# A two-layer block: where the zeros of the expert slots are written, when the 4-bit weights are loaded, and in which order the first sequence goes

## The chip, the core and the metric

The kernel runs on one core of a Trainium2 chip. A core has five engines that run their own instruction streams in order: PE (matrix multiplication), DVE (vector), ACT (activation functions and copies), POOL (general), and SP, which here only issues transfers. Transfers between the chip's main memory and the on-chip memory are carried by 16 DMA engines. An instruction waits where it depends on another engine's or a transfer's result, and everything behind it on its engine waits with it.

The metric is the device time of one execution, in microseconds (us), lower is better.

## The reference

Four sequences of 256 tokens with 256 features go through two layers. Cut to what matters:

```python
# layer 0
x = x + attn0(layernorm(x))      # 16 heads of 16, window of 128, RMS-normalised q and k, rope
x = x + ffn0(layernorm(x))       # weights (1024 x 256 and 256 x 1024) from 4 bits:
                                 #   (q - 7.5) * scale per block of 64, plus a rank-16 product (LoRA)
# layer 1
x = x + scan(layernorm(x))       # selective state space: h_t = exp(dt*A) h_(t-1) + dt*B*x, 16 states
x = x + moe_block(layernorm(x))  # attention with 32 query heads of 128 and 4 key/value heads,
                                 #   then 32 experts, 8 for each token, and a shared expert
```

All arithmetic is float32, apart from some small bf16 operands that hold a value in parts. A sequence's steps depend on each other in that order; the sequences depend on each other only in the expert stage, where tokens are ordered by expert.

## The kernel before

**Streams.** Each piece of the work is a Python generator that yields after a small step: `l0_attention(b)` (24 steps: 4 of projection, 8 that find each row's lowest score, 10 of softmax and values, and the close), `dequantise` (8 pieces that build the feed-forward's float32 weights), `feed_forward(b)` followed by `scan(b)` (together 25 steps for a sequence, `after[b]`), `lower()` (layer 1's attention over all sequences, 16 pairs of heads each, 64 steps) and `zeros()` (35 steps). `timed(stream, start, span, steps)` gives each stream a due time and a pace, and `play` always takes the step that is due first. Times in `timed` are plain numbers that only order the steps; they are not microseconds.

**Planner.** The order in which `play` writes the instructions is a priority. The framework's planner then goes through them with its own model of durations and puts on each engine, at each moment, the instruction of the highest priority that is ready by that model. So an instruction that waits for nothing can be placed far ahead of its place in the program. Buffers come from pools: a tile with `bufs=n` has n buffers in turn, and the next user waits until the last reader is done. Waits are put in by the framework.

**Stages.** First `play`: layer 0's attention of sequence 0 (`first`) and `dequantise` must end, and sequence 1's attention (`second`, `heads[1]`) may advance beside them. Its pool `deq` holds sequence 0's attention buffers and the LoRA factors; when it closes, its memory goes to the pools of layer 1's attention (`l1`) and of the scan (`ssm`), so their first users wait for it. Then the constants of the second layer are loaded (lines 957 to 974). The second `play` (line 1057) holds all else up to the experts: `after[b]`, the attention of sequences 1 to 3 in layer 0 (`heads[1]`, `following(2)`, `following(3)`), `lower()` and `zeros()`. `lower()` runs `after[0]` to its end before its first step, and `after[b + 1]` before it opens the next sequence. Its steps load query weights (`wq`, three buffers) and output weights (`wo`, four).

**Zeros.** The experts work on slots in main memory: 32 x 1024 rows of 289 floats, where each token's row is scattered, and three arrays of sums. All must hold zero before. `zeros()` writes one expert's slots, 1,156 KB, per step, from a tile of 128 x 289 zeros whose rows are repeated by the access pattern. The tile has one buffer, and each step asks for it anew and clears it on POOL (line 706), so each clearing waits until the transfer before it has read the tile. POOL also masks layer 0's probabilities (`l_pr`, lines 362 and 366), adds the rotated parts of queries and keys (302, 567), and scales part of layer 1's probabilities (652).

**Dequantisation.** For each of four pieces of the up weights and four of the down weights, the integers and the scales (broadcast over 64 rows, two transfers) are loaded into two of the eight buffers `g2`, which all of the layer 0 code shares; DVE combines them (lines 219 and 232), PE forms the low-rank product, and DVE adds it.

**Experts.** After the last attention result (line 715 of sequence 3), rows are scattered, a plan is made, and 76 tiles go through a fixed software pipeline (`experts`); then the sums are added. The change doesn't touch this.

Of the kernel before, what the change touches and what calls it, by code (L numbers as in the profile page):

```python
# [8 lines left out]
F32 = mybir.dt.float32  # L9
I32 = mybir.dt.int32  # L10
# [6 lines left out]
P = 128  # L17
# [20 lines left out]
NE = 32  # L38
# [5 lines left out]
ROW = D + NE + 1  # L44
SUMS = 3
PAIRS = NH // 2
# [5 lines left out]
def block_kernel(ctx: ExitStack, tc, out, a):  # L52
    nc = tc.nc
    V, A, G, T = nc.vector, nc.scalar, nc.gpsimd, nc.tensor
# [5 lines left out]
    l1w = ctx.enter_context(tc.tile_pool(name="l1w", bufs=1, side="left"))  # L60
# [8 lines left out]
    def g2(name, dtype=F32):  # L69

        return gen.tile([P, 512], dtype, tag="g2", name=name)

    def halves(t):
        return t.rearrange("p (t d) -> p t d", t=2)
# [31 lines left out]
    for c in (1, 3):  # L106
        G.affine_select(
            out=masks[:, c * P : (c + 1) * P], in_=masks[:, c * P : (c + 1) * P],
# [93 lines left out]
    def dequantise(deq):  # L202
        up_a = load(deq, a["upaT"], [16, D], "up_a")
        up_b = load(deq, a["upb"], [16, FF], "up_b")
        dn_a = load(deq, a["dnaT"], [16, FF], "dn_a")
        dn_b = load(deq, a["dnb"], [16, D], "dn_b")
        dnq = a["dnq"].rearrange("(c p) d -> p c d", p=P)
        dns = a["dns"].rearrange("(c j) d -> j c d", j=2)
        for c in range(2):
            for h in range(2):  # L210
                cols = slice(h * 512, (h + 1) * 512)
                q, s = g2(f"upq{c}_{h}", I32), g2(f"ups{c}_{h}")
                nc.sync.dma_start(out=q, in_=a["upq"][c * P : (c + 1) * P, cols])
                for j in range(2):
                    nc.sync.dma_start(
                        out=s[j * 64 : (j + 1) * 64, :],
                        in_=a["ups"][2 * c + j, cols].partition_broadcast(64),
                    )
                V.scalar_tensor_tensor(s, q, -7.5, s, ALU.add, ALU.mult)
                pl = ps(f"lora_up{c}_{h}")  # L220
                T.matmul(pl, up_a[:, c * P : (c + 1) * P], up_b[:, cols], start=True, stop=True)
                V.tensor_tensor(w_up[:, c, cols], s, pl, ALU.add)
                yield
        for k in range(4):
            q, s = halves(g2(f"dnq{k}", I32)), halves(g2(f"dns{k}"))
            nc.sync.dma_start(out=q, in_=dnq[:, 2 * k : 2 * k + 2, :])
            for j in range(2):
                nc.sync.dma_start(
                    out=s[j * 64 : (j + 1) * 64, :, :],
                    in_=dns[j][2 * k : 2 * k + 2, :].partition_broadcast(64),  # L230
                )
            V.scalar_tensor_tensor(s, q, -7.5, s, ALU.add, ALU.mult)
            pl = halves(ps(f"lora_dn{k}"))
            for i in range(2):
                r = 2 * k + i
                T.matmul(pl[:, i, :], dn_a[:, r * P : (r + 1) * P], dn_b, start=True, stop=True)
            V.tensor_tensor(w_dn[:, 2 * k : 2 * k + 2, :], s, pl, ALU.add)
            yield
# [450 lines left out]
    def project1(h0, po, oT, wo):  # L689
        for i in range(2):  # L690
            for t in range(2):
# [4 lines left out]
                    skip_group_check=True,  # L696
                )

    def zeros():

        fills = [slots[e * CAP : (e + 1) * CAP, :] for e in range(NE)]
        fills += [t[:, :] for t in sums]
        for i, dst in enumerate(fills):
            n = dst.shape[0] // P
            z = l1w.tile([P, ROW], F32, tag="zero", name=f"zero{i}")
            G.memset(z, 0.0)  # L706
            nc.sync.dma_start(
                out=dst.rearrange("(p k) d -> p k d", k=n),
                in_=z[:, 0 : dst.shape[1]].unsqueeze(1).to_broadcast([P, n, dst.shape[1]]),
            )  # L710
            yield

# [193 lines left out]
    def timed(stream, start, span, steps):  # L906

        return [stream, start, span / steps]
# [36 lines left out]
    with tc.tile_pool(name="deq", bufs=1, side="left") as deq:  # L945
        l0_set(deq)
        l0_set(l0)
        first = l0_attention(0)
        ready = dequantise(deq)
        second = l0_attention(1)  # L950
        play(
            [timed(first, 0, 24, 24), timed(ready, 1, 24, 9)],
            [timed(second, 14, 24, 24)],
        )

    wx_dram = a["wxT"].rearrange("(c p) n -> p c n", p=P)
# [56 lines left out]
    def following(b):  # L1013

        for i in range(1, b):
            drained(heads[i])
        yield from heads[b]

    def lower():
        pairs = attention()  # L1020
        drained(after[0])
        for b in range(B):
            for i in range(PAIRS):
                if i == OPEN_AT // 2 and b + 1 < B:
                    drained(after[b + 1])
                if b == B - 1 and i == 0:
                    early.close()
                    scans.close()
                    wres = ctx.enter_context(tc.tile_pool(name="wres", bufs=1, side="right"))
                    end.append(ctx.enter_context(tc.tile_pool(name="end", bufs=1, side="right")))  # L1030
                    wgu.append(wres.tile([P, 2, NE, 2 * P], F32, tag="wgu", name="wgu"))
                if b == B - 1:
                    for c in range(2):
                        for k, w in ((0, "Wg"), (1, "Wu")):
                            nc.sync.dma_start(
                                out=wgu[0][:, c, 2 * i : 2 * i + 2, k * P : (k + 1) * P],
                                in_=a[w][i][:, :, c, :],
                            )
                    if i == PAIRS // 2:
                        sw2 = g2("shared_gu").rearrange("p (k c n) -> p k c n", k=2, c=2)  # L1040
                        for k, w in ((0, "Wsg"), (1, "Wsu")):
                            nc.sync.dma_start(
                                out=sw2[:, k], in_=a[w].rearrange("(c p) i -> p c i", p=P)
                            )
                        sdw = g2("shared_d")[:, 0:D]
                        nc.sync.dma_start(out=sdw, in_=a["Wsd"])
                        shared_w.extend((sw2[:, 0], sw2[:, 1], sdw))
                next(pairs)
                yield
        drained(pairs)  # L1050
# [5 lines left out]
    after = {b: sequence(b) for b in range(B)}  # L1056
    play(
        [
            timed(after[0], 24, 52, 25),
            timed(heads[1], 24, 30, 14),  # L1060
            timed(after[1], 76, 60, 25),
            timed(following(2), 54, 66, 24),
            timed(after[2], 150, 110, 25),
            timed(following(3), 120, 110, 24),
            timed(after[3], 270, 140, 25),
            timed(lower(), 76, 4 * 130, 4 * PAIRS),
            timed(zeros(), 26, 120, NE + SUMS),
        ]
    )

# [156 lines left out]
    for t in range(0, NT, 2):  # L1227
        two = slice(t, t + 2)
        parts = moe.tile([P, SUMS, 2, D], F32, tag="parts", name=f"parts{t}", bufs=2)
        for j in range(SUMS):  # L1230
            nc.sync.dma_start(  # L1231
                out=parts[:, j],
# [113 lines left out]
```

## Time and profile before

| | us |
|---|---|
| median of three runs (1225.37 to 1229.05) | 1225.68 |
| the profiled execution | 1224.67 |
| its span, first to last instruction | 1223.0 |
| PE busy (84% of the span) | 1030.4 |
| DVE busy (63%) | 773.1 |
| ACT busy (37%) | 448.8 |
| POOL busy (37%) | 446.6 |

The transfers move 132.9 MB, a mean of 109 GB/s. In the profile's rows `L706` is a line of the kernel, `out<-in` are names of tiles with numbers left out (`l_pr` is `l0_pr`), `x35` counts instructions, and a bracket at the end of a row gives the idle time of the engine before it and what ended it. PEclk or the last decimal columns give the granted clock of PE as a share of full speed. A wait that is put down to one releaser is the one that came last. `SPq` rows are transfers as SP issues them; where several are joined, the second number runs from the first issue to the last.

Two hand-overs in the trace help to place what follows. The 35 clearings run from 12.0 to 312.0 us, and the transfers out of the cleared tile are issued from 43.6 to 312.3. Layer 1's first query matmul runs at 287.0, its last attention result is added at 1006.1. By sequence, the additions to `x` end at 124.4, 221.7, 385.2 and 586.8 (layer 0 attention), 155.0, 312.0, 485.0 and 676.8 (feed-forward), 268.6, 422.0, 626.0 and 816.7 (scan), and 599.0, 771.5, 904.2 and 1006.1 (layer 1 attention).

### The profile page before, as it was taken

The page shows a single profiled execution, that of the slowest core. Times are in us where ns is not written, and L with a number is a line of the kernel's source. Part 1 is how long each engine was busy: PE and PEld are TensorE (multiplying, and loading weights), DVE is VectorE, ACT ScalarE, POOL GpSimd, SP SyncE. Part 2 cuts the span into 40 slices and gives each one's busy share as a digit, 9 for nine tenths or more (in the row PEclk, how much of TensorE's full clock was granted, in tenths as well). Part 3 has the DMA queues.
Part 4 walks back from the last instruction along what each step waited for, and adds up shares of the span by engine and source line. Part 5 has one row for each costly group of instructions (what it writes and reads, how often), then busy time and mean ns, then how long its engine had stood idle before and what let it go on. Part 6 is the DMA issues. An engine that isn't in the chain of part 4 may idle for free. (4 is left out here: it accounts for less than half of the span.)

```text
span 1223.0 us, 16090 instructions
## 1 busy us (share of the span) xinstructions
PE 1030.4 (84%) x4739; PEld 731.4 (60%) x4739; DVE 773.1 (63%) x2368; ACT 448.8 (37%) x1374; POOL 446.6 (37%) x509
## 2 busy tenths in 40 slices
PE   4887867788899899799999979989999995799880
PEld 2545633336555576566677757667877773677660
DVE  4634236772688873569984588886677643466662
ACT  1030133311454343364444454535454541333320
POOL 4021021011232231242244442346435635388882
PEclk8575866858889899899999989999999997799995
DMA  4667755656201010111122672123333315589876
GB/s 127 191 151 185 193 162 152 161 154 167 95 18 35 27 44 30 31 35 35 52 63 73 197 203 61 53 71 100 98 90 99 100 36 217 120 153 149 146 106 165
DMA packets 130323, 132.93 MB, mean 109 GB/s; under 512 B 10608, under 2 KB 124048, under 8 KB 130224
## 3 DMA queue, kind: packets, MB, share of 16 engines
q1 hardware_dynamic: 116208, 112.34, 32.9%
q0 software_dynamic: 14016, 19.44, 9.1%
q8 instruction: 42, 0.69, 0.2%
q14 instruction: 57, 0.47, 0.1%
HBM read 69.84 MB, written 61.90 MB: 108 GB/s over the span
## 5 line engine op out<-in xcount | busy, mean ns | idle before, releaser
L567 POOL TENSOR_TENSOR at_q_rot<-at_q_t,at_q_t 128x512 f32<-128x512 f32 x64 | 82.1, 1282 | 203.1 <-DVE at_q_t L563 138.8
L642 ACT ACTIVATE at_pr<-at_pr,at_low 128x128 f32<-128x128 f32 (+1 forms) x256 | 113.6, 445 | 70.5 <-DVE at_low L638 69.5
L1189 POOL DMA_INDIRECT sum<-mx_o,at x76 | 118.5, 1559 | 45.5 <-DVE mx_wj L1154 23.1
L693 PE MATMUL at_po<-at_wo,at_oT 128*128 128x256 f32 x512 | 130.4, 381 | 2.5 <-ACT at_oT L686 2.5
L611 PE MATMUL at_pq<-at_hT,at_wq 128*128 128x256 f32 x512 | 126.0, 386 | 1.2 <-ACT at_oT L686 0.9
L652 POOL TENSOR_SCALAR at_pr<-at_pr,at_rden 128x128 f32<-128x128 f32 x128 | 86.5, 685 | 89.6 <-DVE at_rden L647 71.0
L540 PE MATMUL sm_y<-sm_hc,ident 128*128 128x512 f32 x128 | 80.7, 733 | 35.8 <-DVE sm_hc L539 35.3
L611 PEld LDWEIGHTS at_pq<-at_hT,at_wq 128*128 128x128 f32 x512 | 96.8, 193 | 17.9 <-issue 2.8
L693 PEld LDWEIGHTS at_po<-at_wo,at_oT 128*128 128x128 f32 x512 | 93.2, 190 | 15.2 <-ACT at_oT L686 3.2
L563 DVE TENSOR_TENSOR at_q_t<-at_pq,rope 64x512 f32<-64x512 f32 x128 | 88.1, 688 | 8.6 <-POOL at_k_rot L567 6.2
L1140 PE MATMUL mx_pgu<-wgu,mx_xT 128*128 x304 | 82.1, 393 | 6.8 <-DVE mx_act L1165 2.9
L561 DVE TENSOR_TENSOR at_q_t<-at_pq,rope 128x512 f32<-128x512 f32 x64 | 44.0, 687 | 65.4 <-PE at_pq L611 64.3
L638 DVE CUSTOM_DVE_ANT_0 at_pr<-at_sc,masks 128x128 f32<-128x128 f32 (+1 forms) x256 | 77.4, 353 | 9.6 <-PE at_sc L634 7.8
L528 ACT ACTIVATE decay<-sm_dt,na 128x255 f32<-128x255 f32 x128 | 57.3, 499 | 64.2 <-DVE sm_h L534 59.5
L706 POOL MEMSET zero<- 128x289 f32 x35 | 12.0, 344 | 186.8 <-DMA slots<-zero 175.9
L676 ACT COPY at_pT<-at_pb 128x256 f32<-128x256 f32 x64 | 23.5, 367 | 154.1 <-PE at_pb L672 153.9
L853 POOL DMA_INDIRECT slots<-mo_row,mo_at x64 | 64.7, 1011 | 40.4 <-DVE plan_ti L748 20.9
L534 DVE TENSOR_TENSOR_SCAN sm_h<-decay,sm_w 128x512 f32<-128x512 f32 x64 | 78.0, 1236 | 0.7 <-ACT decay L528 0.3
L683 PE MATMUL at_pav<-at_pT,at_v 128*128 128x512 f32 x128 | 70.1, 630 | 8.9 <-DVE at_q_t L563 6.0
L634 PE MATMUL at_sc<-at_k_rot,at_q_rot 128*128 128x256 f32 x256 | 76.5, 380 | 0.0
L336 DVE CUSTOM_DVE_ANT_0 l_junk<-l_sc,masks 128x128 f32<-128x128 f32 (+1 forms) x128 | 40.8, 353 | 36.3 <-PE l_sc L329 33.3
L1188 DVE COPY mx_o<-mx_po 128x256 f32<-128x256 f32 x76 | 32.2, 424 | 48.4 <-DMA sum<-mx_o,at 32.3
(314 smaller groups left out, 2144.6 us busy)
## 6 DMA issues: line engine op xcount, KB each, us to landing
slots<-zero SPq DMA_DIRECT2D x32, 1156.0 KB
at_wq<-in_Wq_dram SPq DMA_DIRECT2D x64, 256.0 KB
at_wo<-in_Wo_dram SPq DMA_DIRECT2D x64, 256.0 KB
xg<-slots SPq DMA_DIRECT2D x76, 144.5 KB
wgu<-in_Wg_dram SPq DMA_DIRECT2D x32, 128.0 KB
wgu<-in_Wu_dram SPq DMA_DIRECT2D x32, 128.0 KB
wd<-in_Wd_dram SPq DMA_DIRECT2D x8, 512.0 KB
sum<-zero SPq DMA_DIRECT2D x3, 1152.0 KB
```

The costliest lines, as they stand in the source:

```text
L534: V.tensor_tensor_scan(hs.rearrange("p c l -> p (c l)"), da.rearrange("p c l -> p (c l)"), w.rearrange("p c l -> p (c l)"), 0.0, ALU.mult, ...
L540: T.matmul(y, ident, hc.rearrange("p c l -> p (c l)"), start=n == 0, stop=n == NS - 1)
L563: V.tensor_tensor(t2[lo : lo + 64], src[hi : hi + 64], sin[hi : hi + 64].unsqueeze(1).to_broadcast([64, n, S]), ALU.mult,)
L567: G.tensor_tensor(dst, t1, t2, ALU.add)
L611: T.matmul(pq[:, i, :], wq[:, c, i * HD : (i + 1) * HD], hT[:, c, :], start=c == 0, stop=c == 1,)
L634: T.matmul(sc[:, P : 3 * P], qT[:, i, P:S], kT[:, 0, :], start=True, stop=True)
L638: V.tensor_tensor_reduce(pr[:, cols], sc[:, cols], mask, 1.0, 3.0e38, ALU.add, ALU.min, low[:, k : k + 1],)
L642: A.activation(pr[:, cols], pr[:, cols], AF.Exp, scale=-1.0, bias=low[:, k : k + 1], accum_out=den[:, k : k + 1],)
L652: scaled.append(G.tensor_scalar(prs[i][:, cols], prs[i][:, cols], rden[:, k : k + 1], None, ALU.mult).ins)
L693: T.matmul(po[:, t, :], oT[:, i, t * P : (t + 1) * P], wo[:, i, :], start=h0 + i == 0 and t == 0, stop=h0 + i == NH - 1 and t == 1, skip_g ...
L1140: T.matmul(pgu, xT[:, c, :], wgu[0][:, c, :, :].rearrange("p e n -> p (e n)")[:, bass.ds(weights[i], 2 * P)], start=c == 0, stop=c == 1,)
L1189: G.indirect_dma_start(out=sums[i % SUMS], out_offset=bass.IndirectOffsetOnAxis(ap=at, axis=0), in_=o, in_offset=None, compute_op=ALU.add,)
```

## The change

Three things. The zero tile is made and cleared once, ahead of `zeros()`, and all 35 transfers read it; the stream comes due at 46 and no longer at 26. `dequantise` issues all 24 of its loads in its first step, into 16 tiles of its own in `deq`, and yields before it uses them; it now has 10 steps, due over 20. The due times change: `second` may begin at 12 and not 14, `after[0]` is due over 20 and not 52, `heads[1]` over 20, `lower()` from 45 and not 76, and the streams of the later sequences around that. The number and kind of all other instructions stay.

```diff
 def dequantise(deq):
...
+        parts = []
         for c in range(2):
             for h in range(2):
                 cols = slice(h * 512, (h + 1) * 512)
-                q, s = g2(f"upq{c}_{h}", I32), g2(f"ups{c}_{h}")
+                q = deq.tile([P, 512], I32, tag=f"upq{c}_{h}", name=f"upq{c}_{h}")
+                s = deq.tile([P, 512], F32, tag=f"ups{c}_{h}", name=f"ups{c}_{h}")
                 nc.sync.dma_start(out=q, in_=a["upq"][c * P : (c + 1) * P, cols])
...
+                parts.append((q, s))
+        for k in range(4):
+            q = halves(deq.tile([P, 512], I32, tag=f"dnq{k}", name=f"dnq{k}"))
+            s = halves(deq.tile([P, 512], F32, tag=f"dns{k}", name=f"dns{k}"))
+            nc.sync.dma_start(out=q, in_=dnq[:, 2 * k : 2 * k + 2, :])
+            for j in range(2):
+                nc.sync.dma_start(
+                    out=s[j * 64 : (j + 1) * 64, :, :],
+                    in_=dns[j][2 * k : 2 * k + 2, :].partition_broadcast(64),
+                )
+            parts.append((q, s))
+        yield
+        for c in range(2):
+            for h in range(2):
+                cols = slice(h * 512, (h + 1) * 512)
+                q, s = parts[2 * c + h]
                 V.scalar_tensor_tensor(s, q, -7.5, s, ALU.add, ALU.mult)
...
         for k in range(4):
-            q, s = halves(g2(f"dnq{k}", I32)), halves(g2(f"dns{k}"))
-            nc.sync.dma_start(out=q, in_=dnq[:, 2 * k : 2 * k + 2, :])
-            for j in range(2):
-                nc.sync.dma_start(
-                    out=s[j * 64 : (j + 1) * 64, :, :],
-                    in_=dns[j][2 * k : 2 * k + 2, :].partition_broadcast(64),
-                )
+            q, s = parts[4 + k]
             V.scalar_tensor_tensor(s, q, -7.5, s, ALU.add, ALU.mult)
...
+    zero = l1w.tile([P, ROW], F32, tag="zero", name="zero")
+    G.memset(zero, 0.0)
+
     def zeros():
...
-        for i, dst in enumerate(fills):
+        for dst in fills:
             n = dst.shape[0] // P
-            z = l1w.tile([P, ROW], F32, tag="zero", name=f"zero{i}")
-            G.memset(z, 0.0)
             nc.sync.dma_start(
                 out=dst.rearrange("(p k) d -> p k d", k=n),
-                in_=z[:, 0 : dst.shape[1]].unsqueeze(1).to_broadcast([P, n, dst.shape[1]]),
+                in_=zero[:, 0 : dst.shape[1]].unsqueeze(1).to_broadcast([P, n, dst.shape[1]]),
             )
             yield
...
-            [timed(first, 0, 24, 24), timed(ready, 1, 24, 9)],
-            [timed(second, 14, 24, 24)],
+            [timed(first, 0, 24, 24), timed(ready, 1, 20, 10)],
+            [timed(second, 12, 24, 24)],
...
-            timed(after[0], 24, 52, 25),
-            timed(heads[1], 24, 30, 14),
-            timed(after[1], 76, 60, 25),
-            timed(following(2), 54, 66, 24),
-            timed(after[2], 150, 110, 25),
-            timed(following(3), 120, 110, 24),
-            timed(after[3], 270, 140, 25),
-            timed(lower(), 76, 4 * 130, 4 * PAIRS),
-            timed(zeros(), 26, 120, NE + SUMS),
+            timed(after[0], 24, 20, 25),
+            timed(heads[1], 24, 20, 12),
+            timed(lower(), 45, 4 * 130, 4 * PAIRS),
+            timed(following(2), 50, 60, 24),
+            timed(after[1], 60, 64, 25),
+            timed(following(3), 120, 100, 24),
+            timed(after[2], 150, 100, 25),
+            timed(after[3], 270, 110, 25),
+            timed(zeros(), 46, 120, NE + SUMS),
```

## The prediction, made before the result was known

> **What bounds the kernel now.** I read the page's slices first, then the busy times of five stretches, then the waits, then the timeline of POOL, PE and SP inside the first 300 us. The slices (one digit for 30.6 us):
>
> ```profile
> PE   4887867788899899799999979989999995799880
> POOL 4021021011232231242244442346435635388882
> PEclk8575866858889899899999989999999997799995
> DMA  4667755656201010111122672123333315589876
> ```
>
> From slice 11 to 33 PE is full at full clock. In the first ten it has gaps, half its time at half clock, while DMA is at 0.5 to 0.7. The stretches are cut at the first query matmul of layer 1 (287.0), the opening of sequence 3's attention (842) and the last attention result (1006). Columns: length, then busy us of PE, its weight loads, DVE, ACT, POOL, then granted clock, DMA share, GB/s.
>
> ```profile
> 0.00:287.00 287.00, 209.87 (x788) 121.55 (x789) 147.65 (x415) 62.29 (x167) 51.72 (x116) 0.68 0.62 162
> 287.00:320.00 33.00, 29.22 (x143) 21.45 (x142) 15.89 (x64) 8.83 (x26) 6.68 (x11) 0.94 0.65 190
> 320.00:842.00 522.00, 476.46 (x2265) 340.39 (x2264) 391.07 (x1019) 241.47 (x742) 176.83 (x199) 0.96 0.22 65
> 842.00:1006.00 164.00, 161.80 (x807) 130.41 (x805) 100.36 (x331) 82.14 (x277) 77.53 (x92) 1.00 0.28 84
> 1006.00:1223.00 217.00, 153.02 (x741) 117.65 (x740) 118.16 (x539) 54.09 (x163) 133.90 (x92) 0.85 0.74 149
> ```
>
> Busy time by clock gives work in full-clock us: 209.9 x 0.68 = 142.7 by 287, then 27.5 + 457.4 + 161.8. So PE loses 144 us of the first 287 and only 72 of the next 719. After 287 PE bounds; before it, something else. The expert stage after 1006 is untouched by the change. What holds the front is in the waits and in the timeline:
>
> ```profile
> POOL zero L706 <- DMA slots<-zero: 175.9, 29, 15.5
> POOL l_pr L362 <- ACT l_pr L357: 61.1, 25, 8.9
> ```
>
> ```profile
> 156.32 0.34 POOL L706 MEMSET zero<- 128x289 f32 x1 [7.38 <-DMA slots<-zero]
> ...
> 163.86 0.34 POOL L706 MEMSET zero<- 128x289 f32 x1 [6.25 <-DMA slots<-zero]
> 164.15 0.63 POOL L362 TENSOR_SCALAR_AFFINE_SELECT l_pr<-l_pr 128x512 f32<-128x512 f32 x1
> ...
> 165.20 1.49 PE L378 MATMUL l_av<-l_pr,l_v 128*32 128x256 f32 x8 [6.69 <-POOL l_pr L366]
> ...
> 166.62 1.12 PE L189 MATMUL sm_pT<-ident,sm_xn 128*128 128x128 f32 x4
> ```
>
> POOL stands at a clearing of the one zero tile until the DMA before it has landed; behind it waits the mask of layer 0's softmax, behind that PE's `l_av`, and behind that, in PE's order, sequence 0's `sm_pT`, whose input was ready at 159.4. On SP (issue times):
>
> ```profile
> 43.55 11.15 SPq L707 DMA_DIRECT2D slots<-zero  x2
> ...
> 65.64 0.62 SPq L226 DMA_DIRECT2D dnq<-in_dnq_dram  x1
> ...
> 133.55 159.59 SPq L707 DMA_DIRECT2D slots<-zero  x22
> 293.24 0.62 SPq L607 DMA_DIRECT2D at_wq<-in_Wq_dram  x1
> ```
>
> The down weights queue behind zeros (the last at 93, used at 101), and the fourth query weight behind 22 of them. Sequence 0's milestones, from the rows of its residual adds: layer 0 attention 124.4, feed-forward 155.0, scan 268.6, first layer 1 query 287.0.
>
> **The change, part by part.**
>
> *Zero tile cleared once.* 34 of 35 clearings go: 34 x 0.34 = 11.6 us of POOL work and its 186.8 us of waiting (175.9 + 10.9 for the sums). POOL isn't the bound; what counts is what stood behind. I take the visible pieces: 6.7 us at `sm_pT` above; about 4 at the last softmax pair of sequence 0 (exponential done at 102.8, mask at 108.4 after a 5.64 us wait; PE filled most of it with other work, so 2 to 6).
>
> *Where the zeros go.* Their due time moves from 26 to 46, but nothing holds a zero DMA any longer, and the order here is made by readiness: the first clearing ran at 12.05 although its place is behind layer 0's first attention, and the first three query weights were issued at 111 to 118 for use at 287. So I expect all 35 on SP in one run behind the constant loads, from about 31 us (SP's 18 early loads end at 12.4; 24 + 17 issues at 0.45 are 18.5 more), not beside the attention. Each takes 0.53 on SP. Once the loads before them have drained (8.9 MB by the sizes of the issues, 33 us at the rate found next), at about 37, one zero of 1,184 kB occupied the DMA engines from 202.8 to 207.2, 4.4 us of a 7.3 us cycle: 269 GB/s. 35 x 4.4 = 154, end near 191. Query weights stand behind: by the Trainium skill, "DMA: Bandwidth & Descriptors", Queues, rings and completion order, each engine consumes descriptors in ring order, which speaks against this change. By the engines' row the first query weight lands at about 193, under the chain below and free. If zeros keep their present pace (312.3 - 43.6 over 34, 7.9 us; 7.5 away from the loads between), it lands at 37 + 35 x 7.5 = 300 and attention waits. I take 4.4, because the gap in each cycle is the very wait that goes; the other end is a rival. If SP meets a query weight among the zeros, it stands at it until `deq` is free, some 119, with the zeros behind it: half of them, 17 x 4.4 = 75, would end at 194, still free.
>
> *Quantised loads in front.* 24 DMAs, 4.2 MB, 15.6 us of engine time, are issued together; 11 of the 17 constant loads that they pass were issued from 14 to 19 and now come at about 24 to 28, the other six near 31 instead of 40 to 43. First uses are at 168 (`wx`) and 280 (`wv`): nothing, covered by 130 us. Without that cover it would be 15.6. What they give: DVE waited 1.5 us at 93 and 2.9 at 101 for down scales, with sequence 0's rotation and values behind it: about 4. Eight general buffers are no longer shared with these tiles; the 32 KB a partition that they take in `deq` are overlaid by tiles first needed after layer 0's first attention: nothing.
>
> *Chain of sequence 0 first.* Two more steps of sequence 1's attention go before sequence 0's end (12 left, not 14): two score steps at half clock, about 2 us each, +4. So layer 0 attention: 124.4 - 4 - 4 + 4, rounded down for the freed buffers, 119. Feed-forward: 30.6 us, of which PE gave about 7 to sequence 1's scores; I take 26: 145. Scan preparation, 155.0 to 193.3, is 38; less the 6.7, and half of the 6.2 in which DVE stood at sequence 1's reciprocal (wait 2.82, run 3.36): 28: 173. The 16 scan steps took 75.3, 4.7 each, with sequence 2's projection and scores among them. Undisturbed, the two steps from 198 ran at 2.3 by DVE, and at half clock PE needs 2.5: floor 40. Sequence 2 now comes due at 50, behind the chain, but sequence 1's softmax still shares PE: between 40 and 75 I take 53: 226. Opening 18.4, taken 17: attention at 243, 44 us earlier.
>
> *What comes back.* Sequence 2's work of 222 to 287 (scores 9.9, query-key 5.6, turns 3.9, values 2.1, transposes 0.6: 22.1 busy at 0.63 = 13.9) goes into the PE-bound stage. Some still fills gaps; I charge 9, at the 0.90 useful share that PE has after 287: 10. Against it, at 312 to 324 PE now loses some 6 us, with POOL at its last clearing and query weights between zeros: that goes.
>
> *The clock.* The Trainium skill, "TensorE: Matmul & The Clock Gate", Part 1, says that sustained busy time of some 3.4 us releases the half clock. Two rows from the front:
>
> ```profile
> 44.00:48.00 4.00, 4.00 (x17) 2.79 (x16) 4.00 (x20) 0.00 (x0) 0.00 (x0) 0.50 0.97 304
> 136.00:140.00 4.00, 4.00 (x17) 3.03 (x18) 1.29 (x8) 0.00 (x1) 0.00 (x0) 1.00 0.79 180
> ```
>
> By the rule the stretch from 36 to 72 would halve once its gaps close, 18 us more gain. By the row, PE was full there and still at 0.50, in matmuls of 16 rows; at 136 with 128-row ones it was at 1.00. I follow the row: no gain of clock in layer 0.
>
> *Sum.* 1223.0 - 44 + 10 - 6 = 1183.0. The profiled execution took 1224.67, 1.7 around its span; the median of the three runs, 1225.68, is 1.0 above that. So 1183.0 + 1.7 + 1.0 = **1186 us**.
>
> **Rivals.**
>
> *The wall of zeros (slower).* The planner thinks the query weights early, puts layer 1's matmuls ahead of other work in PE's order, and they stand until the zeros are through. At 7.5 us a zero that is 300 against 243: 1186 + 57 = 1243. It decides against the change once the weight lands after 243 + 40 = 283, at more than 7.0 us a zero (168 GB/s). For it: stretches with zeros moved only 149 to 190 GB/s. Against: in them the engines stood still 40% of the time. Chance 0.19.
>
> *Only the order moves.* PE bounds from 287 on, so all that is pushed out returns, and the planner already fills by readiness, so due times do little. Only the pieces of waiting are left: 4 + 4 + 6.7 + 6 = 20.7, less the 4 of the two extra steps: 1209, and up to 1222 as more of it returns. For it: PE was over 80% busy from 36 to 124. Chance 0.15, a quarter of it within 0.3%.
>
> *The front warms up.* Without gaps, and with layer 1's 128-row matmuls among layer 0's, the clock holds; attention starts near 215 with most work done: about 1150. Chance 0.12.
>
> **How the numbers follow.** The likeliest, chance 0.54, is 1186, own range 1163 to 1207 (scan 40 to 75, return 0 to 14). 0.3%, 3.7 us, is about what a measurement of this kernel can tell from no change. Faster: 0.54 + 0.12 + 0.11 = 0.77; same 0.04; slower 0.19. The range goes from beyond the warm case, 1142, to where half of the wall case is left out, 1240.
>
> **What would show it.** One clearing on POOL and no wait there; zeros on SP in one run from about 31, DMA at 0.9 or more to about 190; the last down weight multiplied in before 60; sequence 0's adds near 119, 145 and 226; first layer 1 query near 243, with no wait for its weight; useful PE time lost before it about 109 us, not 144; the stretch from there to the last attention result about 723 us; the expert stage 217 as before. The prediction is wrong if that query waits for its weight, if the scan still takes 75, or if PE after it is below 0.88 useful.

## The result, and the profile after

The rows below the median are from one profiled execution of each kernel.

| | before | after |
|---|---|---|
| median of four runs each, us | 1227.37 (1225.37 to 1231.97) | 1212.63 (1208.50 to 1213.68) |
| first query of layer 1 | 287.0 | 239.6 |
| from there to the last attention result | 719.1 | 757.3 |
| last attention result | 1006.1 | 996.9 |
| from there to the end of the span | 216.9 | 213.5 |

The ratio is 0.987, with a 95% interval of 0.983 to 0.991: 15 us faster, where 40 were forecast. Attention starts 47 us earlier (44 were forecast), but only 9 us of that are left at the last attention result. The last 3.4 us lie in the expert stage, which took 211.7 to 219.1 in the kernels of this study though none of them touches it, so they are not put down to the change.

The slices of the changed kernel, 30.3 us to a digit:

```profile
PE   4889868659799979999999989999999995899980
POOL 4021012021132223134235423345435635388882
PEclk8575869779878989989999999999999997899995
DMA  9994999900000101111123276123333316689876
```

DMA is now full in the first eight slices, but for one gap in the fourth, and nearly empty in the ten after them. The first query now falls in slice 8. Behind it, in slices 9 to 15, PE has 5, 9, 7, 9, 9, 9 and 7; in the kernel before, slices 11 to 16, behind its first query, have 8, 9, 9, 8, 9 and 9.

Next the busy times of three stretches, cut at the first query and at the last attention result (columns: length, busy us of PE, its weight loads, DVE, ACT and POOL, then granted clock, DMA share, GB/s). First before, then after:

```profile
287.00:1006.10 719.10, 667.52 (x3212) 492.25 (x3210) 507.34 (x1415) 332.44 (x1044) 261.03 (x301) 0.97 0.25 75
```

```profile
0.00:239.60 239.60, 176.19 (x708) 104.87 (x709) 134.27 (x347) 56.84 (x147) 38.43 (x81) 0.73 0.96 217
239.60:996.90 757.30, 696.73 (x3292) 506.78 (x3291) 520.36 (x1482) 338.12 (x1064) 262.62 (x302) 0.95 0.22 64
996.90:1210.40 213.50, 151.68 (x740) 116.69 (x740) 118.20 (x539) 54.12 (x163) 134.00 (x92) 0.86 0.76 151
```

Busy time by clock, as in the prediction: the front now holds 128.6 full-clock us of work and loses 111 (before: 142.7 and 144). So 14 us of work went behind the first query, and 33 us of loss went from the front. The stretch behind holds 661.9 and loses 95.4, where it held 647.5 and lost 71.6. It grew by 14.4 of work and 23.8 of new loss, together the 38.2 that ate the head start. Of the loss 9 is idle time of PE (60.6 for 51.6) and 15 is clock (34.8 for 20.0). The length and the idle time are measured directly; the border between work and clock is softer, as it multiplies a long stretch by its mean clock. Summed over windows of 4 us the work grew by 18.6 and the loss by 19.6, 10.6 of it clock.

By sequence, layer 1's attention takes 26.7, 9.3, 2.1 and 0.1 us longer than before (its results are added at 578.3, 760.1, 894.9 and 996.9). So nearly all of the growth lies in the first two sequences.

PE's longest waits between the first query and the last attention result, before and after (us in total, times, longest):

```profile
PE sm_y L540 <- DVE sm_hc L539: 22.0, 24, 4.4
...
PE l_av L378 <- POOL l_pr L366: 4.9, 3, 2.9
```

```profile
PE l_ptr L326 <- POOL qpad L314: 19.4, 4, 7.0
PE sm_y L552 <- DVE sm_hc L551: 13.7, 22, 3.2
```

The wait at `l_ptr` is new in this stretch; some of the others became shorter (`sm_y` by 8.3 us, `l_av` by 4.3). `l_ptr` turns the queries and keys of layer 0; it follows a round trip from PE's projection through ACT's squares, DVE's root and rotation and POOL's addition. The timeline of the changed kernel shows one, right after the first query, for sequence 2:

```profile
256.06 1.88 PE L287 MATMUL l_pqk<-wqkv,l_xT 128*128 128x512 f32 x4
...
259.43 0.38 ACT L180 ACTIVATE l_rms_junk<-l_pqk 128x256 f32<-128x256 f32 x1
...
264.97 0.82 POOL L314 TENSOR_TENSOR qpad<-l_t,l_t 128x256 f32<-128x256 f32 x1 [4.18 <-DVE l_t L310]
...
265.85 1.11 PE L326 MATMUL l_ptr<-ident,qpad 128*128 128x128 f32 x4 [7.05 <-POOL qpad L314]
```

PE stands 7 us, with attention's next pairs queued behind `l_ptr` in its order. In the kernel before, this sequence's two round trips lay among the scan steps of sequence 0, which filled them but for 1.3 and 2.5 us:

```profile
234.53 1.12 PE L314 MATMUL l_ptr<-ident,qpad 128*128 128x128 f32 x4 [1.32 <-POOL qpad L302]
```

Three windows of the changed kernel after the first query:

```profile
252.00:260.00 8.00, 6.80 (x25) 4.76 (x24) 3.44 (x12) 3.18 (x13) 1.69 (x2) 0.87 0.11 33
260.00:268.00 8.00, 2.15 (x10) 1.80 (x12) 5.00 (x17) 1.74 (x9) 3.57 (x5) 0.56 0.00 0
268.00:276.00 8.00, 8.00 (x32) 6.24 (x33) 3.05 (x11) 1.02 (x2) 0.00 (x0) 0.59 0.07 18
```

PE is busy for 2.15 of 8 us, and in the next 8, with work for every moment, it has a mean clock of 0.59. This is not the only place: summed over windows of 4 us, of the 28 us that the stretch loses to the clock about 6 lie between 252 and 276, behind the first two of the four waits at `l_ptr` (4.9 and 7.0 us), and about 10 between 324 and 352, where sequence 2's softmax runs. The kernel before has a low stretch of the latter kind too (331 to 347, about 6 us).

The queue of SP in the changed kernel, issue times (a row of several runs from the first issue to the end of the last):

```profile
38.53 41.97 SPq L720 DMA_DIRECT2D slots<-zero  x10
109.38 1.40 SPq L619 DMA_DIRECT2D at_wq<-in_Wq_dram  x3
111.24 1.40 SPq L631 DMA_DIRECT2D at_wo<-in_Wo_dram  x3
112.68 1.97 SPq L720 DMA_DIRECT2D slots<-zero  x2
114.69 3.33 SPq L631 DMA_DIRECT2D at_wo<-in_Wo_dram  x1
118.06 100.69 SPq L720 DMA_DIRECT2D slots<-zero  x20
218.80 15.12 SPq L720 DMA_DIRECT2D sum<-zero  x3
```

```profile
SPq L619 <- DVE qpad L348: 28.8, 1, 28.8
```

The zeros begin at 38.5 and stop while SP stands 28.8 us at the first query weight, until the memory of its buffer is free. From 112.7 on they are issued again, the last until 234; the transfers have drained at about 242. POOL clears once, at 3.0, and waits for no transfer.

### The profile page after: what moved, and what is told of

The parts are those of the page before. It is cut to its first block, busy times and chain, and to the rows that moved or that the text cites. A ratio compares the mean times of both kernels' runs of the same rounds, so it can differ in the third digit from the quotient of the medians.

```text
span 1210.4 us, 15992 instructions
## 1 busy us (share of the span) xinstructions
PE 1024.6 (85%) x4739; PEld 728.3 (60%) x4739; DVE 772.8 (64%) x2368; ACT 449.1 (37%) x1374; POOL 435.0 (36%) x475
## 5 line engine op out<-in xcount | busy, mean ns | idle before, releaser
L623 PE MATMUL at_pq<-at_hT,at_wq 128*128 128x256 f32 x512 | 131.9, 401 | 0.8 <-DVE at_pT L687 0.5
L664 POOL TENSOR_SCALAR at_pr<-at_pr,at_rden 128x128 f32<-128x128 f32 x128 | 83.7, 663 | 89.3 <-DVE at_rden L659 58.2
L623 PEld LDWEIGHTS at_pq<-at_hT,at_wq 128*128 128x128 f32 x512 | 101.0, 202 | 18.2 <-issue 1.9
L552 PE MATMUL sm_y<-sm_hc,ident 128*128 128x512 f32 x128 | 76.1, 697 | 31.8 <-DVE sm_hc L551 31.4
L705 PEld LDWEIGHTS at_po<-at_wo,at_oT 128*128 128x128 f32 x512 | 93.1, 191 | 14.2 <-issue 2.5
L650 DVE CUSTOM_DVE_ANT_0 at_pr<-at_sc,masks 128x128 f32<-128x128 f32 (+1 forms) x256 | 77.4, 354 | 15.1 <-PE at_sc L646 13.2
L374 POOL TENSOR_SCALAR_AFFINE_SELECT l_pr<-l_pr 128x512 f32<-128x512 f32 x32 | 23.5, 733 | 148.9 <-ACT l_pr L369 148.9
## 6 DMA issues: line engine op xcount, KB each, us to landing
sum<-zero SPq DMA_DIRECT2D x3, 1152.0 KB, 17.4
```

What stands on the lines that cost most here:

```text
L552: T.matmul(y, ident, hc.rearrange("p c l -> p (c l)"), start=n == 0, stop=n == NS - 1)
L623: T.matmul(pq[:, i, :], wq[:, c, i * HD : (i + 1) * HD], hT[:, c, :], start=c == 0, stop=c == 1,)
L650: V.tensor_tensor_reduce(pr[:, cols], sc[:, cols], mask, 1.0, 3.0e38, ALU.add, ALU.min, low[:, k : k + 1],)
L664: scaled.append(G.tensor_scalar(prs[i][:, cols], prs[i][:, cols], rden[:, k : k + 1], None, ALU.mult).ins)
L705: T.matmul(po[:, t, :], oT[:, i, t * P : (t + 1) * P], wo[:, i, :], start=h0 + i == 0 and t == 0, stop=h0 + i == NH - 1 and t == 1, skip_g ...
```

## The experiments

The kernel before stood at medians of 1237.2, 1224.7, 1236.2, 1228.8 and 1223.8 us in the five sets, so kernels are compared within a set, and across sets by the profiled places alone, which repeat within 2 us for the changed kernel (last attention result 996.9, 996.8, 995.2) and within 5.4 for the zero tile alone (990.6, 985.2). What each run gave, with profiled places in us:

| kernel | first query | stretch | last attention result | median (before in the same set) |
|---|---|---|---|---|
| zero tile once | 274.8 | 715.8 | 990.6 | 1199.2 (1237.2) |
| loads in front | 294.9 | 728.5 | 1023.4 | 1235.6 (1237.2) |
| due times alone | 249.1 | 771.1 | 1020.2 | 1236.4 (1237.2) |
| zero once, loads, old due times | 269.6 | 716.2 | 985.8 | 1199.6 (1237.2) |
| before | 287.1 | 718.4 | 1005.5 | 1225.1 (1224.7) |
| changed kernel | 239.4 | 757.4 | 996.8 | 1212.9 (1224.7) |
| changed, attention due 76 | 311.1 | 708.4 | 1019.5 | 1236.3 (1224.7) |
| old due times, chain of sequence 0 first | 269.4 | 717.8 | 987.2 | 1205.7 (1224.7) |
| old due times, again | 269.8 | 716.2 | 986.0 | 1202.6 (1236.2) |
| old due times, attention due 45 | 241.8 | 804.3 | 1046.1 | 1257.6 (1236.2) |
| changed, sequence 2 due earlier | 274.3 | 724.1 | 998.4 | 1213.6 (1236.2) |
| changed, zeros after the scan | 236.9 | 757.4 | 994.3 | 1209.6 (1236.2) |
| changed kernel, again | 237.4 | 757.8 | 995.2 | 1209.1 (1228.8) |
| zero tile once, again | 269.6 | 715.6 | 985.2 | 1201.8 (1228.8) |
| old due times, zeros after the scan | 269.2 | 728.5 | 997.7 | 1212.2 (1228.8) |
| chain first, attention due 60 | 257.3 | 739.3 | 996.6 | 1214.1 (1228.8) |
| old due times, attention due 84 | 279.6 | 731.1 | 1010.7 | 1227.5 (1223.8) |
| old due times, attention due 100 | 318.1 | 680.9 | 999.0 | 1219.9 (1223.8) |

**The parts one by one.** Theory G was that the front's gain is given back behind the first query whatever it comes from; rival S, that the steps of the sum hold and another part of the change costs.

Zero tile once:

```diff
+    zero = l1w.tile([P, ROW], F32, tag="zero", name="zero")
+    G.memset(zero, 0.0)
...
-        for i, dst in enumerate(fills):
+        for dst in fills:
...
-            z = l1w.tile([P, ROW], F32, tag="zero", name=f"zero{i}")
-            G.memset(z, 0.0)
```

> Only the zero tile is cleared once; zeros still due at 26, loads and due times as before. Theory G (what the front gains is given back in the stretch after layer 1 opens, because less other work is left over or has been done ahead to fill PE there): the stalls behind POOL go (4 + 6.7 us before the first query, which comes at 270 to 280 instead of 287), about 3 in 10 of it reach the end, as 47 us gave 13: 1221 to 1226. Rival S (the steps of the prediction add up and reach the end; what fails in the whole change is another part): 4 + 6.7 + 6 at 312 to 324 come out whole, about 1210. Rival W (a wall of transfers costs time): zeros run from 30 to beyond 190 without a stop, loads stand behind them, and the time is above 1230.

Ratio 0.9685 (0.965 to 0.972). This refutes G: the gain is not given back. As a time it is larger than S had it, 38 us, but the kernel before stood high in this set; at the last attention result, against the other sets' profiles of the kernel before, it is 15.5 us. Loads in front, then (24 loads in the generator's first step, ten steps over 24):

```diff
-            [timed(first, 0, 24, 24), timed(ready, 1, 24, 9)],
+            [timed(first, 0, 24, 24), timed(ready, 1, 24, 10)],
```

> Only the quantised loads go in front, all 24 in one step. Theory G: DVE's 4 us for the down scales go, of which some 1 us reaches the end: 1224 to 1228. Rival S: 4 us whole, 1223. Rival W: the 4.2 MB in front delay other first loads by up to 15.6 us: 1231 to 1240.

Ratio 1.000 (0.998 to 1.002): nothing; G's 1 us fits, S's 4 us lies beyond the interval. The time is among those that rival W named, but only because the whole set stood higher. All due times of the change, with a clearing for each zero:

```diff
-            timed(after[0], 24, 52, 25),
+            timed(after[0], 24, 20, 25),
...
-            timed(lower(), 76, 4 * 130, 4 * PAIRS),
+            timed(lower(), 45, 4 * 130, 4 * PAIRS),
...
```

> Only the due times change (clearing on POOL for each zero, loads as before). Theory G: layer 0 and scan of sequence 0 come earlier, first query at 255 to 265; as the stretch after it loses more of PE, 1216 to 1222. Rival S: the 29 us that the chain was expected to gain by order alone reach the end less 10 returned: about 1206. A further rival: POOL's clearings stand in the chain all the same and nothing is gained, 1224 to 1232.

Ratio 0.999 (0.998 to 1.001). The first query came at 249, earlier than G had it, and nothing of it reached the end: neither number held. The further rival's "nothing is gained" did, though not for its reason, as the chain of sequence 0 did come earlier. In this kernel POOL's clearings stand in the round trip described above:

```profile
PE l_ptr L314 <- POOL qpad L302: 37.3, 4, 15.7
```

```profile
267.95 0.34 POOL L706 MEMSET zero<- 128x289 f32 x1 [4.94 <-DMA slots<-zero]
268.25 0.72 POOL L302 TENSOR_TENSOR qpad<-l_t,l_t 128x256 f32<-128x256 f32 x1
```

This makes it a test of that round trip. Its due times are those of the changed kernel, and the loads, which differ too, gave nothing by themselves. The first two waits at `l_ptr` are 14.1 and 15.7 us here and 4.9 and 7.0 in the changed kernel; the other two are 4.0 and 3.4 in both, and PE's next longest wait hardly differs (`sm_y`, 14.2 for 13.7). With 17.9 us more of this wait PE is idle 18.9 us longer in the stretch (79.5 for 60.6), and the stretch is 13.8 us longer (771.1 for 757.3). So most of what PE waits there is lost at the end of the stretch.

The whole change but for the due times:

```diff
-            timed(after[0], 24, 20, 25),
+            timed(after[0], 24, 52, 25),
...
-            timed(lower(), 45, 4 * 130, 4 * PAIRS),
+            timed(lower(), 76, 4 * 130, 4 * PAIRS),
...
```

> The zero tile cleared once and the loads in front, but every due time as before. Theory G: first query at 265 to 278, time 1220 to 1225; the order of the streams then carries most of the 15 us of the whole change. Rival S: 20 us whole, about 1206, and the new due times cost some. If it comes out at 1212 or below, the due times gave nothing although they brought the first query 30 us forward.

Ratio 0.970 (0.966 to 0.973), below 1212 as the last sentence allowed for: the due times brought the query 30 us forward and gave nothing.

**Which due time.** The kernel before, and the changed one beside two that share a part of its due times:

> The kernel before, for its profile on the chip of this set. Theory Z (clearing the tile once is worth some 35 us because POOL's clearings delay layer 0 of every sequence as long as zeros are written): the zeros end later than 312 and the first query comes later than 287 where the time is above 1226, by about as much as the time is. Rival: the extra time lies in the stretch from the first query to the last attention result (719) or in the expert stage (217).

It stood at 1225 here, so theory Z could not be tried on it. That the zeros are slower where the time is higher fits two kernels of the first set that clear for each zero (last zero at 332.1 and 329.5, here 311.5), but no profile of the kernel before was taken there, so this stays open.

> The changed kernel beside the others. Theory D (its new due times cost what part of the zero tile gains): ratio to the kernel before 0.98 to 0.99, while the same without the new due times had 0.970. Rival (the two chips differ, the due times cost nothing): 0.965 to 0.973.

Ratio 0.991 (0.987 to 0.994), theory D at its upper edge.

```diff
-            timed(lower(), 45, 4 * 130, 4 * PAIRS),
+            timed(lower(), 76, 4 * 130, 4 * PAIRS),
```

> The changed kernel with one number put back: layer 1's attention due from 76, not 45. Theory E (the early due time is what costs: attention's matmuls stand among layer 0's of sequence 2 before the rest has a lead): first query later than 240, at 250 to 265, sequence 2's attention of layer 0 ends before 385, and the ratio is 0.965 to 0.976. Rival F (the chain of sequence 0 placed first costs, by leaving the other sequences' work behind): as the changed kernel, 0.98 to 0.99.

Ratio 1.009 (1.006 to 1.011), slower than either theory. With the later streams' new due times, attention from 76 falls behind them and opens at 311.

```diff
 # zero tile once, loads in front, and of the due times:
-            [timed(first, 0, 24, 24), timed(ready, 1, 24, 10)],
-            [timed(second, 14, 24, 24)],
+            [timed(first, 0, 24, 24), timed(ready, 1, 20, 10)],
+            [timed(second, 12, 24, 24)],
...
-            timed(after[0], 24, 52, 25),
-            timed(heads[1], 24, 30, 14),
+            timed(after[0], 24, 20, 25),
+            timed(heads[1], 24, 20, 12),
```

> Zero tile once and loads in front, and of the new due times only those that put sequence 0's chain first (the first stage's, after[0] over 20, heads[1] over 20); attention and the later streams due as before. Theory E: the chain gains 15 to 30 us at the first query against the kernel with all old due times (269.6), and half or more of it reaches the end: ratio 0.955 to 0.968. Rival F: 0.98 to 0.99, since the chain first leaves sequence 2's work behind. In between, equal to the old due times (0.967 to 0.973): the chain first is worth nothing, its gain is all returned work.

Ratio 0.985 (0.983 to 0.988). Two rows of PE's timeline in this kernel, the end of sequence 0's scan and the first query:

```profile
222.41 1.12 PE L559 MATMUL sm_py<-ident,sm_yT 128*128 128x128 f32 x4 [0.68 <-ACT sm_yT L555]
...
269.39 0.81 PE L623 MATMUL at_pq<-at_hT,at_wq 128*128 128x256 f32 x3
```

The scan is added at 223.6, 28 us earlier than with the old due times (251.5), and the first query comes at 269.4, as with them (269.6): in the 47 us between lie the end of sequence 1's layer 0 attention and sequence 2's projections and scores, which otherwise ran beside the scan. The last attention result is within 1.4 us of that kernel's. So placing the chain first gives nothing by itself; it moves work from one side of the scan to the other.

> Zero tile once and loads in front with every due time as before, again, since the kernel before took 1237 beside it the first time and 1225 beside the changed kernel. Theory H (the waits that go are worth 20 us at the last attention result; the new due times cost some 11 of them there): ratio 0.976 to 0.984, 6 to 15 us faster than the changed kernel's 1213. Rival: the 0.970 of the first time holds, 0.967 to 0.974. Rival (due times cost nothing): 0.987 to 0.993.

Ratio 0.973 (0.971 to 0.975), between theory and first rival as a ratio (the kernel before stood at 1236 again); in us it is 10 below the changed kernel's 1213. Then attention early, alone:

```diff
 # zero tile once, loads in front, all else due as before
-            timed(lower(), 76, 4 * 130, 4 * PAIRS),
+            timed(lower(), 45, 4 * 130, 4 * PAIRS),
```

> As the kernel with every due time as before, but layer 1's attention due from 45, not 76. Theory H1 (attention placed early is what costs, since it displaces sequence 2's and sequence 1's steps of layer 0, and PE is emptier and colder after the first query): first query at 240 to 250, the stretch from it to the last attention result 745 to 760 instead of 716, time 5 to 15 us above the kernel with the old due times, near 1212. Rival H2 (the other streams' due times cost): the same as with the old due times within 4 us.

The direction is H1's, the size far beyond it: ratio 1.016 (1.014 to 1.019), 55 us slower than the same kernel with attention due from 76. The first query comes 28 us earlier, and the stretch behind it has these rows (the attention stretch in this kernel, then with the old due times):

```profile
241.80:1046.10 804.30, 716.02 (x3326) 515.30 (x3325) 528.54 (x1493) 339.23 (x1067) 264.78 (x304) 0.93 0.20 60
```

```profile
269.80:986.00 716.20, 666.22 (x3212) 491.21 (x3210) 505.78 (x1415) 332.25 (x1044) 258.57 (x297) 0.97 0.22 67
```

By busy time and clock 20 of the 88 us are work that came back (665.9 for 646.2); 68 are PE standing idle (88.3 for 50.0) or at lower clock (50.1 for 20.0). It is not the same wait alone: `l_ptr` has 13.2 us in this stretch and `at_pT`, layer 1's own input, 17.5; with the old due times neither is among PE's waits there.

```diff
-            timed(following(2), 50, 60, 24),
+            timed(following(2), 30, 40, 24),
```

> The changed kernel with sequence 2's layer 0 attention due from 30 over 40, not from 50 over 60. Theory H: PE's work is a sum that the order only moves; the first query comes later (265 to 285) and the stretch after it shrinks by as much: last attention result 985 to 1000, time 1203 to 1215. Rival (an early first query is worth its time): every us of delay at the first query shows at the end, 1235 to 1250.

As theory H said: the first query 35 us later, the stretch 33 shorter, the last result 1.5 us later. A head start of 35 us was worth 1.5.

**The wall of zeros.** In the changed kernel the zero tile is made from `x` after the scan, so that no zero can be written before:

```diff
-    G.memset(zero, 0.0)
...
+        G.tensor_scalar(
+            zero, x.rearrange("p t d -> p (t d)")[:, 0:ROW], 0.0, None, ALU.mult
+        )
         for dst in fills:
```

> The changed kernel, but the zero tile is made from x on POOL after sequence 0's scan, so that all zeros are written beside layer 1's first attention and none before. If the zeros in front are free: the first query comes as in the changed kernel, 236 to 242. If they slow the front (transfers full to 240): before 232. Behind it, query and output weights stand among zeros: by the pace of 5.1 us a zero and 2 to 5 zeros between weights, each pair of 13 to 17 us waits little or up to 25 us for its weight for some 180 us: time 1215 to 1245. If it is at 1213 or below, the wall of zeros costs nothing wherever it stands.

```profile
0.00:236.90 236.90, 173.81 (x708) 103.69 (x709) 134.03 (x347) 56.79 (x147) 39.02 (x81) 0.74 0.23 60
236.90:994.30 757.40, 696.75 (x3292) 507.06 (x3291) 520.62 (x1482) 337.97 (x1064) 262.14 (x302) 0.95 0.45 114
```

The DMA share of the front falls from 0.96 to 0.23, and the first query comes 0.5 to 2.7 us earlier than in the changed kernel's three profiles; with all the zeros beside attention that stretch is the same to 0.4 us. There the zeros cost nothing in either place. The same edit with the old due times (zeros due at 77), an attempt at a better kernel:

> Zero tile once and loads in front with the old due times, and the zeros only after sequence 0's scan (the tile is made from x then, zeros due at 77), as an attempt at a better version than both. From the run that moved the zeros in the changed kernel: 2 to 3 us earlier at the first query (267 instead of 269.7), the same stretch after it (716), time 1195 to 1202. If the query weights between zeros are late here: the stretch 725 or more.

Here the stretch grew by 12 us. SP's queue and PE's order show it, in the timeline of this kernel:

```profile
398.35 15.77 SPq L722 DMA_DIRECT2D slots<-zero  x3
414.22 5.40 SPq L619 DMA_DIRECT2D at_wq<-in_Wq_dram  x1
```

```profile
429.11 2.47 PE L623 MATMUL at_pq<-at_hT,at_wq 128*128 128x256 f32 x5 [10.72 <-DMA at_wq<-in_Wq_dram]
```

A query weight was issued behind three zeros and came 10.7 us late. So the wall exists; in the changed kernel no query weight was late by it.

**In one set, and between the due times.**

> The changed kernel, to stand in one set with those that share a part of it. By theory H its last attention result is at 997 and its time 8 to 14 us above that of the zero tile alone, although its first query comes 35 us earlier. Rival (the earlier sets differ in something else): within 4 us of it.

> The zero tile cleared once alone, in one set with the changed kernel. Theory H: last attention result at 990 to 992, time 1197 to 1206, faster than the changed kernel by 0.5 to 1.1%. Rival (the whole change is better than this part): slower than it.

The changed kernel 0.984 (0.981 to 0.987), the zero tile alone 0.979 (0.976 to 0.982): 1209.1 (six runs, 1207.0 to 1212.8) against 1201.8 (1198.9 to 1202.5, one at 1209.4), 7 us or 0.6% apart, and 10 us at the last attention result. The one-part kernel is the better of the two.

```diff
 # as the kernel with the chain of sequence 0 first
-            timed(lower(), 76, 4 * 130, 4 * PAIRS),
+            timed(lower(), 60, 4 * 130, 4 * PAIRS),
```

> The chain of sequence 0 first and the later streams as before, with attention due from 60: between 45 and 76. Theory H: the first query moves to 245 to 260 and the stretch after it grows by as much or more; last attention result 987 (as with 76) or later, up to 1020. Rival (an early first query is worth its time if the later streams are left as they were): 965 to 980.

As H said: 12 us earlier at the first query, 22 longer behind it. Last, later due times in the kernel with the old ones (84 and 100 in place of 76):

> Zero tile once, loads in front, old due times, but attention due from 84, not 76. An earlier due time (60, 45) made the last attention result later by 9 to 60 us. If the cause is that attention runs before the other sequences have their steps done, a later due time gives the same or a little more: first query 272 to 285, last attention result 980 to 988, time 1195 to 1203. If 76 lies where the two costs balance: 988 to 1000, time 1203 to 1215.

> The same with attention due from 100. By the first case: first query 285 to 305, last attention result 980 to 992. By the second: 1000 to 1025, as PE has the chains' gaps to bear for longer with nothing to fill them.

Ratios 1.002 (1.001 to 1.004) and 0.997 (0.996 to 0.998): they lose all or nearly all of what the zero tile gained. So it is not true that attention should only start later. By due time the last result is 997 (60, with the chain first), 986 (76), 1011 (84) and 999 (100). This is no smooth balance; of the two expectations neither held for 84, and for 100 the second missed by 1 us. Why 84 is the worst of the four was not found; each due time gives another order on every engine.

## Why the prediction was right or wrong

*Direction and range* were right: faster, and 1212.6 lies in 1142 to 1240. It lies outside the likeliest case's own range, 1163 to 1207; the time is that of the rival "only the order moves" (1209 to 1222).

*Zero tile cleared once*: right. 4 + 6.7 + 6 = 16.7 us were forecast; alone it brought the last attention result from 1006.1 to 990.6 and 985.2, 15.5 and 20.9 us. The parts were a little otherwise: 12.2 and 17.4 ahead of the first query for 10.7, and only 3.3 and 3.5 of the 6 behind it. In medians the gain was 38 and 27 us. Some 5 of the 27 lie in the expert stage (212.0 for 216.9); for the 38 there is no profile of the kernel before in its set, so where the rest lay is open.

*Where the zeros go*: one run to 191 was wrong; the case named beside it came instead, with SP standing at a query weight, until 109 rather than 119. The pace was 5.1 us each and not 4.4 (1,184 kB, 232 GB/s for 269), and the transfers ended at about 242 and not 194. Free as forecast: the run without zeros in front gains at most 2.7.

*Quantised loads in front*: cost nothing, as forecast; the gain of 4 wasn't there (1.000 alone; 1199.6 and 1199.2 with and without them beside the zero tile). DVE's two waits for down scales are gone, yet the last down weight is ready at 97 (106 before, and before 60 by the forecast): its low-rank product comes as late as the order of the steps puts it.

*Chain of sequence 0 first*: its milestones were right, 119.8, 145.7, 222.6 and 239.6 against 119, 145, 226 and 243; the useful loss before the first query was 111 us, forecast 109. Counted as in the prediction, the scan's preparation took 22.5 us for 28 and its 16 steps 54.4 for 53, so two small misses cancel. No gain of clock in layer 0 was nearly right too: 0.58 from 36 to 72, with PE busy for 32 of 36 us, 0.53 before; the 18 us of the other reading did not come.

*What comes back* is **the step that failed**. It charged 10 us, 9 of work at a useful share of 0.90, took 6 off, and so had 723 us from the first query to the last attention result; 757.3 it was. These 34 us are more than the whole error: the front came 3.4 us earlier and the expert stage took 3.5 less than forecast. The work that came back was 14.4 (18.6 by the finer windows). The larger part was never in the sum, which charged the returned work 1 us of loss: 23.8 (19.6) of new loss. Sequence 2's layer 0 attention no longer lies in the gaps of sequence 0's scan, where its round trips cost little, but between attention's pairs, where PE stands at `l_ptr`. The useful share fell to 661.9 / 757.3 = 0.874, below the 0.88 that the text named as a sign of being wrong. The reading it began with, PE full at full clock from slice 11 on, was too round: those slices read 7 to 9, and at a useful share of 0.90 there was room to lose more. The runs that move only the order show the same sign: the first query from 274 to 239 is worth 1.5 us, from 269 to 257 costs 9, from 270 to 242 costs 60. That waits at `l_ptr` lengthen the stretch is shown by the kernel with due times alone, where longer ones did. How much of the 23.8 us is theirs is not shown: 9 is idle time, in which 19.4 at `l_ptr` stand against shorter waits elsewhere, and of the lower clock only about 6 us lie right behind them. The rest of the clock's part stays open.

*The expert stage* of 217: 213.5, within its scatter.

*The rivals.* "Only the order moves" had the time and the pieces of waiting (20.7 us forecast; 20.9 in the second run of the zero tile alone), but for a reason that fails: it held that due times do little. They moved the last result by up to 60 us; here together they cost 7 in time and 10 to 11 at the last result, so that the time met the rival's is luck. "The wall of zeros" did not happen in this change and did in one experiment, as one late query weight. "The front warms up" had nothing for it.

## What to carry to other kernels

Where an engine is full later on, an earlier start of that stage is no gain by itself: sum what the engine loses (length less busy time by clock) over both sides of the start, and charge the moved work with the waits it had hidden under its old neighbours. Take a change apart before judging its parts; here one buffer written once beat the whole. An order made by due times and a planner answers to small numbers in jumps, so each setting has to be measured.

## What the runs showed of the hardware

An issue of one zero transfer took SP 0.53 us in the kernel before, where one was under way at a time, and 5.1 us (median) in the changed kernel, where each landed 21.6 us after its issue, so about four were under way (21.6 / 5.1). What stands behind such issues in SP's queue is late before its own transfer begins: the query weight above took SP 5.4 us to issue and PE started its product 14.9 us after the issue began, where such a weight lands in a median of 2.8.

PE's clock can stay low through long stretches of unbroken work. In the kernel before PE was busy for all of 44.0 to 56.9 us at 0.50, with matmuls of 16 rows alone. In the changed kernel it worked without a pause from 265.9 on, after having been idle for 6 of 8 us, and stood at 0.50 for more than 8 us: first transposes and matmuls of 16 rows, then the first query matmuls with 128. Its matmuls, and the clock at the end of this stretch (the third number from the end):

```profile
267.74 1.97 PE L341 MATMUL l_sc<-l_kT,l_qT 16*128 16x128 f32 x8
269.64 1.11 PE L189 MATMUL ff_pT<-ident,ff_xn 128*128 128x128 f32 x4
270.55 3.62 PE L623 MATMUL at_pq<-at_hT,at_wq 128*128 128x256 f32 x8
```

```profile
273.00:274.00 1.00, 1.00 (x4) 0.73 (x4) 0.00 (x0) 0.00 (x0) 0.00 (x0) 0.50 0.00 0
274.00:275.00 1.00, 1.00 (x6) 0.95 (x5) 0.78 (x2) 0.00 (x0) 0.00 (x0) 0.71 0.00 0
275.00:276.00 1.00, 1.00 (x9) 0.90 (x8) 0.99 (x2) 0.00 (x0) 0.00 (x0) 1.00 0.55 145
```

The clock rose some 4 us after the first 128-row query matmul and more than 8 us after the work began. Which of the two it follows was not tried.
